# A perceiver block on one core: the last quarter of the last attention unit transposed on TensorE, four weight pairs loaded at once, and layer norms placed ahead of split halves

## The chip, the cores and the metric

The kernel runs on one core of a Trainium2 chip. The metric is the device time of one execution in microseconds, the median of several runs. The core's engines work side by side, each through its own queue in order: TensorE (PE in the profile; PEld is its weight load), VectorE (DVE), ScalarE (ACT), GpSimd (POOL) and SyncE (SP, which here only issues DMAs).

## The reference, cut to what matters

Three layers with residuals are computed for 512 tokens of width 1024: a cross attention whose queries, keys, values and attention weights are rounded to 8-bit levels, a causal self attention with rotary positions, and a feed-forward layer with 4-bit weights.

```python
x = x + xattn(layernorm(x), ctx, ...)   # 8192 keys, 16 heads of 64; then @ Wp + bp
x = x + attn(layernorm(x), ...)         # 4 sequences of 128, 16 heads; Wq, Wk, Wv, Wo
x = x + ffn(layernorm(x), ...)          # gate and up 1024 -> 2816, silu(gate) * up, down, rms norm

# inside xattn
attn = softmax(q @ k.T)                 # per head
attn = round(attn / s).clip(0, 255) * s # s = max(attn) / 255 of each row
out  = attn @ v
```

## The kernel before, in words

**Stages.** Up to about 1503 us keys and values of the 8192 context rows are projected and quantised. From 1503 to about 2166 us the cross attention runs in 64 units, one for each head `h` and each tile `t` of 128 tokens. Then come ten "parts" (`PARTS`), each a product of the 512 tokens with one 1024 x 512 half of a weight: parts 0 and 1 are the two halves of Wp, 2 the first half of Wv, 3 to 6 halves of Wq and Wk, 7 the second half of Wv, 8 and 9 the halves of Wo. From about 2503 us the feed-forward part runs: 22 rounds of gate and up, then down.

**A unit of the attention.** Its 8192 keys are eight groups of 1024 (`g`). `scores` makes the scores of a group; `exponentials` makes 4096 of them at a time into int16 levels `a`. The levels, read as the bits of a 16-bit float, must be transposed before they multiply the values. Quarters 0 and 2 of the keys are transposed by PE (`transposes`, two 16-bit levels moved as one 32-bit word, L830, copied to SBUF by ACT or DVE at L836), quarters 1 and 3 (`DMA_KC`) by DMA (`dma_transposes`, L845, issued on SP). `values` (L858) multiplies them. The loop over steps `s` writes the order out: `transposes` runs LAG_T = 12 and `values` LAG_V = 18 steps after `scores`. After the last scores only the tail of the last units is left; into its steps `FIRST_AT` puts eight single products of part 0 (`first_step`, L941).

**The parts.** From `with tc.manual_schedule()` on, an agenda fixes the order: `do(step, function, ...)` notes a time for each piece, and `perform` issues the pieces in the order of these times, so they are the order of every engine's queue, and not a time that anything waits for. A step is one k-chunk of 128 of one product; a part has 32 steps, `g = s + 8 t` is where tile `t` of a part begins and `e = g + 8` where it ends.

Weights come in pairs of k-chunks. `load_pair` loads 512 KB into one of two buffers `w_raw` (SP, L1028), `split_pair_hi` splits off the high part on ACT (`sw_h`, L155), `split_pair` the low part and the difference on DVE (`sw_l`, `sw_d`, L158 and L159), with six buffers of each. Three products of reduced precision then stand for one of full precision (`product_step`, L1100, accumulators `acc_a` and `acc_b`, two of each). The tokens are split in the same manner into `x3` (high, low, difference). Part 0 is the exception: it is done in full precision (L941), while `first_split` and `first_difference` (L1072) prepare the split tokens for part 1.

After parts 1 and 9 a tile is joined to the residual (L1111, L1112), its statistics are taken (L1126), and `normalise` writes the norm `xn` (L1131 to L1137). Later `xn_transposes` transposes it on PE (L1080, eight transposes into two PSUM tiles `pt` of three), takes the high halves on ACT (L155) and the low halves and differences on DVE (L158, L159, four instructions); `scale_low` scales the low part on ACT (L1087). Before the change each tile's `xn_transposes` stood 7.5 steps after the tile's end, which is just before the next tile's last half step and so before its norm:

```python
do(e + 0.4, normalise, t)
do(e + 7.5, xn_transposes, t)
do(e + 8.35, scale_low, t)
```

`first_gate_up` (L1253) is the first gate and up product of the feed-forward part; it needs the split norms of all four tiles. After the agenda, pools for the feed-forward part are opened where the pools of the parts were; `load_ffn` loads a weight (`fw_raw`, L1378) and splits it at once (`fw_h`, `fw_l`, `fw_d`). In this last section the order on the engines is found by a scheduler.

Of the kernel before, what the change touches and what calls it, by code (L numbers as in the profile page):

```python
# [34 lines left out]
F32 = mybir.dt.float32  # L35
# [11 lines left out]
P = 128  # L47
# [8 lines left out]
KC = 2048  # L56
# [7 lines left out]

FIRST_AT = (5, 6, 7, 14, 15, 17, 17, 17)
DMA_KC = (1, 3)
# [20 lines left out]
def tile_perceiver(  # L87
# [646 lines left out]
    with tc.tile_pool(name="at_e", bufs=1) as at_e, tc.tile_pool(  # L734
# [8 lines left out]
        for i in range(2):  # L743
            nc.vector.tensor_scalar_mul(sqs[:, i], sq, 1.0 - 2.0 * i)
        vqs = {}

# [77 lines left out]
        def transposes(n, g):  # L824
# [9 lines left out]

            copy = nc.scalar.copy if n < len(units) - 2 or g < 2 and n < len(units) - 1 else nc.vector.tensor_copy
            copy(aT, pt.bitcast(I32))  # L836
# [3 lines left out]
        def dma_transposes(n, c):  # L840

            at_key = c * KC % EC
            a = state[n]["a"][c * KC // EC][:, at_key : at_key + KC].bitcast(F16)
            aT = at.tile([P, KC // P, P], F16, name="aT_d", tag="aT_d", bufs=3)
            nc.sync.dma_start_transpose(out=aT, in_=a)  # L845
            for g in range(KC // SC):
                state[n]["aT", KC // SC * c + g] = [
                    aT[:, g * (SC // P) + i, :] for i in range(SC // P)
                ]

        def values(n, g):
# [105 lines left out]
        with tc.manual_schedule():  # L957
            for s in range(n_steps + LAG_V):
# [4 lines left out]
                if g == NSC // NEC and 1 <= n <= len(units):  # L963
                    dma_transposes(n - 1, DMA_KC[0])
                if g == 0 and 2 <= n <= len(units) + 1:
                    dma_transposes(n - 2, DMA_KC[1])
# [17 lines left out]
                if at_step(s - LAG_V):  # L984
                    values(*at_step(s - LAG_V))
                for fn, *args in meanwhile.get(s - n_steps, ()):
                    fn(*args)
# [33 lines left out]
    def load_pair(h, kp):  # L1021

        raw = sa_f.tile([P, 2, 512], F32, name="w_raw", tag="w_raw", bufs=2)
        if h < len(PARTS):
# [148 lines left out]
    def rotary_transposes(h, t, tag, bufs):  # L1173
        f = live.pop(("f", h, t))
        pt = sa_ps.tile([P, 4, P], F32, name="pt", tag="pt", bufs=3)
        for i in range(4):
            nc.tensor.transpose(pt[:, i, :], f[:, ts(i, P)], ident)
        fT = live[tag, t] = sa_f.tile([P, 4, P], F32, name=tag, tag=tag, bufs=bufs)
        nc.scalar.copy(fT, pt)
# [95 lines left out]
    with tc.manual_schedule():  # L1275
# [10 lines left out]
        for h, (w, n) in enumerate(PARTS):  # L1286
            s = PART * h

            if h > 0:
                for kp in range(NC // 2):  # L1290
                    at = s + {1: (-28, -22, -16, -10), 2: (-37, -33, -6, -3)}.get(h, (-26, -16, -6, -3))[kp]
                    do(at - 9.5, load_pair, h, kp)
                    do(at - 2.5, split_pair_hi, h, kp)
                    do(at + 0.5, split_pair, h, kp)
# [12 lines left out]
            for t in range(NT):  # L1307
# [17 lines left out]
                elif h == 1:  # L1325
                    do(e + 0.2, join_residual, h, t, n)
                    do(e + 0.3, stats, t, 1)
                    do(e + 0.4, normalise, t)
                    do(e + 7.5, xn_transposes, t)
                    do(e + 8.35, scale_low, t)  # L1330
                elif h in (2, 7):
# [38 lines left out]

    with tc.tile_pool(name="ff_t", bufs=2) as ff_t, tc.tile_pool(name="ff", bufs=1) as ff:
        hT = [ff.tile([P, 512], F32, name=f"hT{j}", tag=f"hT{j}") for j in range(NI)]
        ss = ff.tile([P, NT, 2], F32, name="ss")

        def load_ffn(src, n):

            raw = ff_t.tile([P, C], F32, name="fw_raw", tag="fw_raw")
            nc.sync.dma_start(out=raw.rearrange("p (i n) -> p i n", n=n), in_=src)  # L1378
# [18 lines left out]
        def split_inner(pool, j):  # L1397
# [178 lines left out]
```

## Time and profile before

| | us |
|---|---|
| median of 3 runs | 2870.38 (2868.08 to 2871.28) |
| the profiled execution | 2872.01 |
| its span | 2870.2 |
| PE busy | 2661.8 (93%) |
| DVE busy | 2421.4 (84%) |
| ACT busy | 1266.0 (44%) |
| end of the last score on DVE | 2147.3 |
| last product with the values | 2166 |
| first product of part 1 | 2198.2 |
| first product of part 2 | 2230.8 |
| first gate and up product | 2490.25 |
| first product of the loop of the feed-forward part | 2503 |

Times within the execution are counted from the start of its span. The busy shares are means over stages with different limits; what a change in one stage is worth is read from that stage. In a row of the timeline the bracket at the end gives the engine's idle time before the row and the instruction that ended it.

### The profile page before, as it was taken

Reading aid. Unit: us, or ns where it says so; the run is one execution under the profiler, and the core shown is the slowest. Engines: PE = TensorE matmul, PEld = TensorE weight load, DVE = VectorE, ACT = ScalarE, POOL = GpSimd, SP = SyncE. Lnnn points to the kernel's source line nnn. Section 1 sums busy time; section 2 is a strip of 40 time slices with the busy share of each in tenths; the row PEclk is TensorE's granted clock in tenths of the full one; section 3 lists DMA queues with packets and bytes.
Section 4 is the critical chain, followed back from the end, with each engine's and each line's share of the span. In section 5 each row is a group of like instructions: output and inputs, shape, how many; then the busy total and the mean of one; then the engine's idle time right before and its main releaser. Section 6 shows DMA issues by size and latency. Waiting matters only on the chain.

```text
span 2870.2 us, 41035 instructions
## 1 busy us (share of the span) xinstructions
PE 2661.8 (93%) x15480; PEld 2065.8 (72%) x15480; DVE 2421.4 (84%) x3959; ACT 1266.0 (44%) x1400; POOL 455.9 (16%) x608
## 2 busy tenths in 40 slices
PE   8999999999999999999997778877778899899998
PEld 3788888888888888888874555555555677688886
DVE  6899999555699988889879999999996898776674
ACT  4211212121323333333218999999993244333332
POOL 0011111000012222222122333223311000000000
PEclk9999999999999999999998999999999999899999
DMA  5555566222447776777437888778774221122222
GB/s 187 174 194 200 200 212 209 99 90 101 136 119 206 190 194 182 194 180 195 112 90 150 159 168 163 162 152 157 153 145 137 88 78 60 52 96 96 91 93 96
DMA packets 452710, 413.17 MB, mean 144 GB/s; under 512 B 356952, under 2 KB 361624, under 8 KB 452512
## 3 DMA queue, kind: packets, MB, share of 16 engines
q1 hardware_dynamic: 404928, 252.22, 35.9%
q0 software_dynamic: 46528, 157.29, 17.0%
q8 instruction: 121, 1.98, 0.3%
q10 hardware_dynamic: 1056, 1.05, 0.2%
q14 instruction: 77, 0.63, 0.1%
HBM read 220.14 MB, written 104.34 MB: 113 GB/s over the span
## 4 chain that ended last, share of the span: by engine, by line
PE 72%; DVE 19%; issue 4%; POOL 2%; DMA 1%; ACT 1%; DVEq 0%; ACTq 0%; SPq 0%; POOLq 0%
PE kv_a L342 33%; PE kv_b L342 16%; DVE e L787 13%; PE acc_a L1100 3%; PE gate_a L165 3%; PE up_a L165 3%; PE y_a L1463 3%; PE q_ps L292 2%; POOL sk L760 2%; PE acc_b L1100 2%; PE up_b L165 1%; PE gate_b L165 1%; PE y_b L1463 1%; PE a_pt L830 1%; PE sc L780 1%
## 5 line engine op out<-in xcount | busy, mean ns | idle before, releaser
L342 PE MATMUL kv_a<-w_h,c_h 128*128 128x512 f32 x2048 | 806.4, 394 | 0.0
L342 PE MATMUL kv_a<-w_l,c_l 128*128 128x512 f32 x2048 | 806.0, 394 | 0.2 <-ACT w_l L246 0.2
L342 PE MATMUL kv_b<-w_d,c_d 128*128 128x512 f32 x2048 | 806.0, 394 | 0.0
L787 DVE CUSTOM_DVE_ANT_0 e<-sc,sk 128x1024 f32<-128x1024 f32 x512 | 593.6, 1220 | 11.4 <-PE sc L780 10.3
L815 ACT ACTIVATE a<-e,m,sqs 128x4096 int16<-128x4096 f32 x128 | 486.9, 3804 | 27.9 <-DVE m L804 27.6
L342 PEld LDWEIGHTS kv_a<-w_l,c_l 128*128 128x128 f32 x2048 | 384.8, 188 | 89.6 <-ACT w_l L246 0.6
L342 PEld LDWEIGHTS kv_a<-w_h,c_h 128*128 128x128 f32 x2048 | 384.9, 188 | 88.9 <-issue 0.2
L342 PEld LDWEIGHTS kv_b<-w_d,c_d 128*128 128x128 f32 x2048 | 384.8, 188 | 88.9 <-DVE c_d L159 0.3
L155 ACT ACTIVATE c_h<-c_raw 128x1024 fp32r<-128x1024 f32 x128 | 135.1, 1056 | 424.2 <-PE kv_a L342 417.0
L356 DVE SCALAR_TENSOR_TENSOR f<-kv_a,bkv 128x512 f32<-128x512 f32 x256 | 175.8, 687 | 163.4 <-PE kv_a L342 162.7
L780 PE MATMUL sc<-kt,qT 64*128 64x512 bf16 x1024 | 207.0, 396 | 103.6 <-DVE mx L787 99.1
L581 ACT CAST kst<-kT 128x512 bf16<-128x512 int16 x128 | 89.4, 699 | 313.6 <-DMA kT<-ki 313.2
L830 PE MATMUL a_pt<-ident,a 128*128 128x128 f32 x1024 | 178.0, 299 | 20.8 <-ACT a L815 16.1
L357 DVE SCALAR_TENSOR_TENSOR f<-kv_b,f 128x512 f32<-128x512 f32 x256 | 176.7, 690 | 20.3 <-DVE f L356 0.9
L760 POOL PARTITION_BROADCAST sk<-sk_row x120 | 142.7, 1297 | 314.1 <-DVE mx L787 314.1
L830 PEld LDWEIGHTS a_pt<-ident,a 128*128 128x128 f32 x1024 | 113.8, 147 | 87.3 <-ACT a L815 48.3
L780 PEld LDWEIGHTS <-qT 64*128 64x128 bf16 x1024 | 74.9, 93 | 131.7 <-issue 101.3
L158 DVE TENSOR_TENSOR fw_l<-fw_raw,fw_h 128x1024 fp32r<-128x1024 f32 x64 | 78.2, 1222 | 99.8 <-ACT fw_h L155 99.6
L158 DVE TENSOR_TENSOR c_l<-c_raw,c_h 128x1024 fp32r<-128x1024 f32 x128 | 155.7, 1217 | 4.8 <-ACT c_h L155 4.4
L159 DVE SCALAR_TENSOR_TENSOR c_d<-c_l,c_raw 128x1024 fp32r<-128x1024 f32 x128 | 156.3, 1221 | 2.3
L155 ACT ACTIVATE fw_h<-fw_raw 128x1024 fp32r<-128x1024 f32 x64 | 67.7, 1060 | 174.6 <-PE y_a L1463 72.0
L548 ACT CAST vq<-vi 128x1024 f16<-128x1024 int16 x64 | 66.9, 1046 | 170.7 <-DVE vi L541 135.8
(204 smaller groups left out, 4110.1 us busy)
## 6 DMA issues: line engine op xcount, KB each, us to landing
c_raw<-in_ctxT SPq DMA_DIRECT2D x128, 512.0 KB, 3.6
v_d<-f POOLq DMA_DIRECT2D x64, 512.0 KB, 3.1
vl<-v_d POOLq DMA_DIRECT2D x64, 512.0 KB, 4.2
gu_d<-w_ffn POOLq DMA_DIRECT2D x44, 512.0 KB, 3.1
fw_raw<-gu_d SPq DMA_DIRECT2D x42, 512.0 KB, 3.2
k_d<-kst POOLq DMA_DIRECT2D x128, 128.0 KB, 3.5
vq_d<-vq POOLq DMA_DIRECT2D x32, 512.0 KB, 5.0
kt<-k_d SPq DMA_DIRECT2D x64, 256.0 KB, 3.5
```

Source lines behind the costliest of these rows:

```text
L155: nc.scalar.mul(hi, src, 1.0 - 0.5 / UP)
L158: nc.vector.tensor_tensor(lo, src, hi, ALU.subtract)
L159: nc.vector.scalar_tensor_tensor(df, lo, -1.0 - UP, src, ALU.mult, ALU.add)
L165: nc.tensor.matmul(ps, lhsT=lhs(i, k), rhs=rhs(i, k), start=(k == 0 and i != 1), stop=(k == NC - 1 and i != 0),)
L342: nc.tensor.matmul(ps, lhsT=tokens[s][i][:, k, :], rhs=w3[s < KT][k][i][:, ts(n, 512)], start=(k == 0 and i != 1), stop=(k == NC - 1 and i ...
L356: nc.vector.scalar_tensor_tensor(f, a, 1.0 + 1.0 / UP, bias[s < KT][n], ALU.mult, ALU.add)
L357: nc.vector.scalar_tensor_tensor(f, b, -1.0 / UP, f, ALU.mult, ALU.add)
L760: nc.gpsimd.partition_broadcast(tile_of_scales(h, g), sks_at[h][32 * c : 32 * c + 1, ts(half, SC)], channels=P)
L780: nc.tensor.matmul(ps[:, ts(i, 512)], lhsT=qT[rows, h, ts(t, P)], rhs=kts[h, g // 2][rows, ts(g % 2, 512)], start=True, stop=True,)
L787: nc.vector.tensor_tensor_reduce(out=state[n]["e"][-1][:, ts(g % (NSC // NEC), SC)], in0=ps, in1=sks_at[h, g], scale=1.0, scalar=LOWEST, o ...
L815: nc.scalar.activation(a, st["e"][c], AF.Exp, bias=st["m"], scale=sqs[:, 0, t, h : h + 1], accum_out=sums[h][:, t, c : c + 1],)
L830: nc.tensor.transpose(pt[:, i, :], a[:, at_word + P * i : at_word + P * i + P], ident)
```

## The change

- The fourth quarter of the last unit is no longer transposed by DMA. `last_transposes` multiplies it on PE with a 16-bit identity (`ident16`, copied once before the attention), in four groups of four blocks; the levels come out as fractions in PSUM and are scaled back to int16, groups 0 and 2 on DVE, 1 and 3 on ACT. The copy of group 5 of the last unit goes from DVE to ACT.
- Two of the first steps of part 0 move four steps forward (`FIRST_AT`, 14 and 15 to 10 and 11).
- All four weight pairs of part 1 are loaded together ahead of the other pieces; pairs 2 and 3 get one buffer of their own, which is later the place of the transposed queries `qT`, now one tile in place of four. The splits of pairs 1 and 2 of part 1, and of pairs 0 and 1 of part 2, get other times.
- `xn_transposes` and `scale_low` get later times in parts 1 and 9, so that the norm of the next tile comes first.
- The feed-forward pools are cut differently: `fw_raw` and the first ten tiles `hT` get pools of their own.

```diff
-FIRST_AT = (5, 6, 7, 14, 15, 17, 17, 17)
+FIRST_AT = (5, 6, 7, 10, 11, 17, 17, 17)
...
+        ident16 = small.tile([P, P], F16, name="ident16", tag="ident16", bufs=1)
+        nc.scalar.copy(ident16, ident)
...
-            copy = nc.scalar.copy if n < len(units) - 2 or g < 2 and n < len(units) - 1 else nc.vector.tensor_copy
+            by_act = n < len(units) - 2 or (n, g) == (len(units) - 1, 5) or g < 2 and n < len(units) - 1
+            copy = nc.scalar.copy if by_act else nc.vector.tensor_copy
...
+        def last_transposes(q):
+            n, c = len(units) - 1, DMA_KC[1]
+            at_key = c * KC % EC + 512 * q
+            a = state[n]["a"][c * KC // EC][:, at_key : at_key + 512].bitcast(F16)
+            if q == 0:
+                aT = at.tile([P, KC // P, P], I16, name="aT_l", tag="aT_d", bufs=3)
+                state["last"] = aT
...
+            pt = at_ps.tile([P, 4, P], F32, name="a_pt", tag="a_pt")
+            for i in range(4):
+                nc.tensor.matmul(
+                    pt[:, i, :], lhsT=a[:, ts(i, P)], rhs=ident16, start=True, stop=True
+                )
+            scale = nc.vector.tensor_scalar_mul if q % 2 == 0 else nc.scalar.mul
+            scale(state["last"][:, ts(q, 4), :], pt, F16_UNITS)
...
-                if g == 0 and 2 <= n <= len(units) + 1:
+                if g == 0 and 2 <= n <= len(units):
                     dma_transposes(n - 2, DMA_KC[1])
...
+                if n == len(units) + 1 and 1 <= g <= KC // 512:
+                    last_transposes(g - 1)
...
-        raw = sa_f.tile([P, 2, 512], F32, name="w_raw", tag="w_raw", bufs=2)
+        if h == 1 and kp >= 2:
+            if kp == 2:
+                live["raw"] = sa_f.tile([P, 2, 2, 512], F32, name="w_raw2", tag="qT")
+            raw = live["raw"][:, kp - 2]
+        else:
+            raw = sa_f.tile([P, 2, 512], F32, name="w_raw", tag="w_raw", bufs=2)
...
-        fT = live[tag, t] = sa_f.tile([P, 4, P], F32, name=tag, tag=tag, bufs=bufs)
+        if tag == "qT":
+            if t == 0 and h == 3:
+                live["q"] = sa_f.tile([P, NT, 4, P], F32, name=tag, tag=tag)
+            fT = live[tag, t] = live["q"][:, t]
+        else:
+            fT = live[tag, t] = sa_f.tile([P, 4, P], F32, name=tag, tag=tag, bufs=bufs)
...
-                    at = s + {1: (-28, -22, -16, -10), 2: (-37, -33, -6, -3)}.get(h, (-26, -16, -6, -3))[kp]
-                    do(at - 9.5, load_pair, h, kp)
+                    at = s + {1: (-28, -24, -13.8, -10), 2: (-35, -31, -6, -3)}.get(h, (-26, -16, -6, -3))[kp]
+                    do(-9.3 if h == 1 else at - 9.5, load_pair, h, kp)
...
-                    do(e + 7.5, xn_transposes, t)
-                    do(e + 8.35, scale_low, t)
+                    do(e + 9.5, xn_transposes, t)
+                    do(e + 10.4, scale_low, t)
...
-                        do(e + 7.5, xn_transposes, t, True)
-                        do(e + 8.35, scale_low, t)
+                        do(e + (9.5, 9.5, 8.6, 7.5)[t], xn_transposes, t, True)
+                        do(e + (10.4, 10.4, 8.7, 8.35)[t], scale_low, t)
...
-    with tc.tile_pool(name="ff_t", bufs=2) as ff_t, tc.tile_pool(name="ff", bufs=1) as ff:
-        hT = [ff.tile([P, 512], F32, name=f"hT{j}", tag=f"hT{j}") for j in range(NI)]
+    with tc.tile_pool(name="ff_t", bufs=2) as ff_t, tc.tile_pool(
+        name="ff_a", bufs=1
+    ) as ff_a, tc.tile_pool(name="ff_raw", bufs=2) as ff_raw, tc.tile_pool(name="ff", bufs=1) as ff:
+        inner_pool = [ff_a if j < EARLY + 2 else ff for j in range(NI)]
+        hT = [inner_pool[j].tile([P, 512], F32, name=f"hT{j}", tag=f"hT{j}") for j in range(NI)]
...
-            raw = ff_t.tile([P, C], F32, name="fw_raw", tag="fw_raw")
+            raw = ff_raw.tile([P, C], F32, name="fw_raw", tag="fw_raw")
...
-            df = ff.tile([P, 512], F32R, name=f"h3_d{j}", tag=f"hT{j}")
+            df = inner_pool[j].tile([P, 512], F32R, name=f"h3_d{j}", tag=f"hT{j}")
```

More of the change, by code (lines that the diff above doesn't have):

```diff
@@ L849, in dma_transposes @@
                 ]
+        def last_transposes(q):
[5 more added lines that the diff above has]
+                state["last"] = aT
+                for g in range(KC // SC):
+                    state[n]["aT", KC // SC * c + g] = [
+                        aT.bitcast(F16)[:, g * (SC // P) + i, :] for i in range(SC // P)
+                    ]
+            pt = at_ps.tile([P, 4, P], F32, name="a_pt", tag="a_pt")
[5 more added lines that the diff above has]
+            scale(state["last"][:, ts(q, 4), :], pt, F16_UNITS)
         def values(n, g):
```

## The prediction

> **What bounds the kernel now.** I read the busy times by stretch first, then what TensorE (PE) waited for from the end of the attention on, then single rows of the timelines around those waits. By stretch (the columns are busy us and instructions of PE, its weight loads, DVE, ACT, POOL, then the granted clock, the DMA share and GB/s):
>
> ```profile
> 2151.00:2204.00 53.00, 43.86 (x233) 25.14 (x233) 30.19 (x33) 22.19 (x25) 13.48 (x11) 0.90 0.59 187
> 2204.00:2257.00 53.00, 44.70 (x194) 35.92 (x195) 43.05 (x65) 14.48 (x21) 0.00 (x0) 0.94 0.18 56
> 2257.00:2459.00 202.00, 193.35 (x1054) 157.62 (x1054) 180.56 (x243) 81.82 (x202) 11.79 (x8) 0.99 0.23 76
> 2459.00:2503.00 44.00, 30.26 (x131) 24.23 (x130) 27.13 (x43) 11.91 (x19) 0.00 (x0) 0.81 0.14 48
> 2503.00:2738.00 235.00, 235.00 (x1008) 189.03 (x1007) 162.83 (x192) 84.41 (x115) 0.00 (x0) 1.00 0.26 91
> ```
>
> The change touches 2151 to 2257 (end of attention, parts 0 to 2) and 2459 to 2503 (last part, first gate and up). There PE is idle 9.1, 8.3 and 13.7 us, at reduced clock, while the feed-forward loop after it is full: PE 235.00 of 235.00. So a microsecond by which that loop starts earlier is a microsecond of the whole. Who holds PE up there:
>
> ```profile
> PE pt L1080 <- DVE xn L1137: 21.0, 6, 6.5
> PE acc_a L941 <- issue: 5.1, 1, 5.1
> PE acc_b L1100 <- DVE x_d L1072: 2.5, 1, 2.5
> PE av L858 <- DMA aT_d<-a: 1.8, 1, 1.8
> ```
>
> and the rows with those waits in brackets:
>
> ```profile
> 2162.69 0.64 PE L858 MATMUL av<-vq,aT_d 128*128 128x64 f16 x16 [1.79 <-DMA aT_d<-a]
> 2181.84 5.75 PE L941 MATMUL acc_a<-wp,xoT 128*128 128x512 f32 x8 [5.07 <-issue]
> 2205.03 2.56 PE L1100 MATMUL acc_b<-sw_d,x_d 128*128 128x512 f32 x8 [2.54 <-DVE x_d L1072]
> 2222.06 1.06 PE L1080 MATMUL pt<-ident,xn 128*128 128x128 f32 x8 [1.30 <-DVE xn L1137]
> 2230.01 1.06 PE L1080 MATMUL pt<-ident,xn 128*128 128x128 f32 x8 [1.29 <-DVE xn L1137]
> 2241.36 1.94 PE L1080 MATMUL pt<-ident,xn 128*128 128x128 f32 x8 [4.67 <-DVE xn L1137]
> 2479.90 1.94 PE L1080 MATMUL pt<-ident,xn 128*128 128x128 f32 x8 [6.00 <-DVE xn L1137]
> 2488.31 1.95 PE L1080 MATMUL pt<-ident,xn 128*128 128x128 f32 x8 [6.47 <-DVE xn L1137]
> ```
>
> One more 1.27 at 2467. The 5.07 is called issue, but the join of acc(0,0) frees the accumulator at 2181.73 on DVE (L1117); it stands behind x_l(0), that behind ACT's x_h(0), that behind the split of weight pair 2, whose load waits for its buffer:
>
> ```profile
> 2151.74 10.61 SPq L845 DMA_TRANSPOSE aT_d<-a  x2
> 2163.57 1.72 SPq L1028 DMA_DIRECT2D w_raw<-in_xWp  x2
> 2174.23 2.76 SPq L1028 DMA_DIRECT2D w_raw<-in_xWp  x2
> 2177.87 1.06 ACT L155 ACTIVATE sw_h<-w_raw 128x1024 fp32r<-128x1024 f32 x1 [5.28 <-DMA w_raw<-in_xWp]
> ```
>
> All these waits together are 30.4 us of 2870: that is the room.
>
> **The change part by part.**
>
> *Last quarter on PE.* One DMA transpose goes (its 3.82 us on SP, 2158.54 to 2162.36); 16 products with an fp16 identity and four scalings come. No row shows this product. Bounds: eight 128x64 fp16 products take 0.41 us, four fp32 transposes 0.66, so 0.8 to 2.6 for the 16; I take 1.1, nearer to the fp16 row. Each scaling is near an aT copy, 0.69 on DVE or 0.58 on ACT; both are nearly idle there. The wait of 1.79 is not for the removed transfer: it is for the second quarter, issued at 2151.74 and landing after 10.9 us, while wp and x load. It stays; but two first steps (0.94 each) now come before it, with three of the four groups. PE then reaches that point at about 2163.5, after the landing at 2162.65. So 1.8 goes, 1.1 comes: PE is at the last transposes of xo at 2167.8 instead of 2168.64, **0.8** gained. wp's second half lands 9.5 after 2148.7, at 2158.2, before the moved steps need it.
>
> *Four pairs at once.* SP has issued the second quarter at about 2158.4 (10.61 less the last 3.82), so the loads go out some 5 us earlier, pairs 2 and 3 in a buffer of their own (qT's slot, unused until part 3). The split of pair 2 moves behind the first two tiles' splits on ACT and DVE. I replay the queues with the trace's durations: xoT copies done at 2169.9; sw_h twice; DVE pairs 2 x 2.45; x_l(0) 1.22; join 0.68: the accumulator is free at 2177.5 instead of 2181.7. PE stands still 1.5 instead of 5.07, and is **4.2** ahead there (the 0.8 included). What is late next: the weights of part 2, pair 1, now stand between the differences x_d(0) and x_d(1) on DVE. In place of 2.54 before acc_b(1,0) I get 0.8 there and 3.0 before (1,1): **-1.3**.
>
> *Norms ahead, part 1.* Each transpose of xn moves behind two further steps (6 products of 0.234 = 1.4 us), and on DVE the norm of tile t+1 (join to xn, 3.85 us, L1111 to L1137) comes before the four split halves of tile t (2.75). That covers 1.30 and 1.29; the 4.67 becomes 0.9, plus 0.9 for a PSUM buffer of `pt` not yet split, and the join of (2,0), now behind the halves, holds up (2,2) by 2.7. 7.26 becomes 4.5: **+2.8**. Parts 3 to 8 get the same work in the same order; the replay carries the lead through unchanged.
>
> *Norms ahead, last part.* Replay, in the times of before, the front's lead not yet taken off: xn(1) at 2463.4, then the last weight pair (2.45) and the halves of tile 0, xn(2) at 2471, in time for PE, which comes to it at 2473. xn(3) is done at 2477.3 instead of 2488.2. But on ACT the scaling of tile 2 stands before x_h(3), so the first gate and up starts at about 2482.8 instead of 2490.25: 7.5, and with the trace's short wait inside it (5.23 for products worth 3.75 at full clock) **8**. Here the new pools matter: the first fw_raw loads stood behind the release of w_raw at 2469.43, their four DVE splits ahead of xn; now they wait for PE too and their splits come after x_d(3). A load takes 3.2, splitting one weight 1.06 + 2.4: ready near 2490 against the first gate at 2495. Cover 5 us; if gone, the excess is lost one to one.
>
> *Clock.* After a wait the trace shows half clock: 0.50 in 2182 to 2186, 0.52 in 2208 to 2210, 0.50 in 2242 to 2244; the waits of 1.3 left 1.00. The 8 records at 2181.84 took 5.75 against 3.5 for their like at full clock. I count 2.2 + 1.9 + 1.4 = 5.5 us lost so in the first region. [...] But here 2.54 was enough; so I charge two leftovers with 1.9 each: **+1.7**. At the end both versions run some products cold: 0.
>
> *At nothing:* the identity's copy (one ACT copy before the first exponentials), the query tile in one piece (same bytes and order), hT in another pool (same order in the loop).
>
> Sum: 4.2 - 1.3 + 2.8 + 8 + 1.7 = 15.4. The profiled execution took 2872.0 (span 2870.2), so 2856.6 there; it is 1.6 above the median, 2870.4, so the median forecast is **2855**.
>
> **Rivals.**
> *Only one side pays.* DVE does 43 of 53 us in parts 1 and 2, so it may be the bound: 30.4 us of waiting would merely change names. Then the end alone gives 8: 2862. If instead fw_raw is released late and eats the end's gain, the front's 7.4 alone: 2863. For it: 3.0 and 2.7 already reappear. Against: DVE itself waits some 15 us between 2168 and 2246, mostly for ACT, behind pair 2.
> *More than replayed.* The leftover waits don't arise and the clock stays up: of 30.4 + 5.5, 22 is won: 2848.
> *Nothing measurable.* The burst of 2 MB meets wp, x and the second quarter's transpose (DMA share above 1.0 at 2152 to 2164), so the weights land no sooner, and fw_raw costs the end: within 6 us of 2870.
> *Slower.* The pools of the feed-forward part are cut anew. If a tile there falls on one released later, the wait recurs in each of 21 rounds of fw_raw loads. The loop has no slack on PE; each microsecond per round costs 21. From 0.75 us per round it eats my 15.4; at 1.2 it gives 2880. Against it: the order of loads and splits in the loop and the number of buffers stay the same, and DVE has 72 us spare in 235.
>
> **How the numbers follow.** A measurement of this kernel tells 0.2% (5.7 us) from no change. Forecast 0.66, one side 0.17, more 0.05, nothing 0.05, slower 0.07. The first three are faster by over 0.2%, less a little of the one-sided case: faster 0.87, same 0.06, slower 0.07. The forecast's own bounds (identity products 1.5 either way, cold stretches 4, leftovers 3) give 2849 to 2861; to hold 8 in 10 with the one-sided case the range is 2847 to 2865.
>
> **What would show it.** Right: no DMA wait on av at the end; the wait before the first xoT step near 1.5; the 4.67, 6.00 and 6.47 gone or under 2.5; first gate near 2488. A second-quarter landing later than 2164, an accumulator wait over 4 in part 2, or a wait of gate_a for fw_h would show a step wrong; a feed-forward loop longer than 235 the slower rival.

## The result, and the profile after

The changed kernel took 2857.37 us (median of 5 runs, 2854.13 to 2859.43) against 2871.28 for the kernel before in the same comparison: a ratio of 0.9951, 95% interval 0.9937 to 0.9966. A second comparison, made with the last experiments, gave 2856.77 against 2873.02, a ratio of 0.9941 (0.9926 to 0.9955). So the change gains 14 to 16 us (the interval of the first comparison reaches from 10 to 18), more than the 0.2% that can be told; 2855 was forecast.

The profiled execution took 2854.13 us, with a span of 2852.4. The first view is the one that the prediction opened with: busy us and instructions of PE, its weight loads, DVE, ACT and POOL, the granted clock, the DMA share and GB/s. The stretches run between nearly the same places of the program as those shown of before: the third boundary lies ten products later in the program and the fourth six.

```profile
2147.40:2195.60 48.20, 41.22 (x249) 23.54 (x249) 29.12 (x32) 23.78 (x28) 13.89 (x11) 1.00 0.55 187
2195.60:2247.70 52.10, 47.45 (x204) 37.25 (x205) 46.27 (x68) 13.80 (x21) 0.00 (x0) 0.93 0.21 63
2247.70:2450.00 202.30, 192.31 (x1050) 156.98 (x1050) 180.35 (x244) 81.72 (x202) 12.74 (x8) 0.99 0.24 77
2450.00:2485.50 35.50, 28.38 (x125) 22.60 (x124) 26.57 (x42) 11.35 (x18) 0.00 (x0) 0.86 0.17 60
2485.50:2720.50 235.00, 235.00 (x1008) 189.03 (x1007) 162.77 (x192) 84.56 (x115) 0.00 (x0) 1.00 0.27 91
```

The first stretch went from 53.0 to 48.2 us and its clock from 0.90 to 1.00; the fourth went from 44.0 to 35.5, of which six products (1.4 us) are the boundary's. The feed-forward loop did not move, and the long third stretch hardly. What PE waits for, in total us, times and the longest (from 2140 on; some smaller rows and one that is as before are left out):

```profile
PE pt L1207 <- DVE f L1201: 9.8, 4, 4.9
PE pt L1110 <- DVE xn L1167: 5.5, 2, 4.5
PE acc_b L1130 <- DVE x_d L1102: 3.8, 2, 3.5
...
PE acc_a L1288 <- ACT x_h L155: 1.8, 1, 1.8
PE acc_a L1130 <- DVE v L1141: 1.7, 1, 1.7
PE acc_a L964 <- DMA wp<-in_xWp: 1.6, 1, 1.6
...
PE acc_a L964 <- issue: 1.6, 1, 1.6
```

The waits for xn fell from 21.0 to 5.5 us, the 5.1 of the first xoT step to 1.6, and the wait of av for the DMA transpose is gone. The wait for a rotary f now heads the list, and one of 1.6 for the weights wp of part 0 is new; it is taken up below. The rows behind the list, each with its wait in brackets:

```profile
2156.83 0.39 PE L868 MATMUL a_pt<-ident,a 128*128 128x128 f16 x4
...
2173.76 3.67 PE L964 MATMUL acc_a<-wp,xoT 128*128 128x512 f32 x8 [1.56 <-issue]
...
2196.61 3.78 PE L1130 MATMUL acc_b<-sw_d,x_d 128*128 128x512 f32 x8 [3.54 <-DVE x_d L1102]
...
2201.46 0.79 PE L1130 MATMUL acc_b<-sw_d,x_d 128*128 128x512 f32 x1 [0.21 <-DVE x_d L1102]
...
2264.27 1.08 PE L1207 MATMUL pt<-ident,f 128*128 128x128 f32 x4 [4.92 <-DVE f L1201]
...
2468.32 1.09 PE L1110 MATMUL pt<-ident,xn 128*128 128x128 f32 x4 [4.48 <-DVE xn L1167]
...
2472.51 5.49 PE L1288 MATMUL acc_a<-x_h,sw_h 128*128 128x512 f32 x16 [1.78 <-ACT x_h L155]
```

**How the executions are compared.** Two profiles of unlike executions should not be laid side by side by absolute time. The kernel after was already 3.56 us ahead at 2148.06, at the end of the exponentials of the last unit's first half, ahead of all changed code but the one copy of `ident16` (before: 2151.62). In its second profile that place was at 2152.75, and over the fourteen profiles it lay from 2146.9 to 2154.4, so the lead belongs to the one execution. I therefore count from that place: the *front* runs from it to the transposes of the last rotary f of part 6, the *end* from there to the first gate and up product (2490.09 before; the 2490.25 in the table ahead is 0.16 late), and the last column gives the loop's first gate, counted from it too.

| kernel | first xoT step | first rotary f | front | end | first gate |
|---|---|---|---|---|---|
| before | 30.2 | 122.0 | 240.7 | 97.8 | 351.2 |
| after | 25.7 | 116.2 | 233.9 | 90.6 | 337.2 |
| after, second profile | 25.3 | 114.8 | 233.3 | 90.6 | 336.7 |
| front alone | 25.6 | 116.1 | 234.4 | 97.9 | 344.7 |
| end alone | 29.5 | 123.8 | 240.5 | 90.6 | 343.8 |
| end, norms alone | 31.2 | 125.1 | 242.8 | 95.8 | 351.3 |
| four pairs alone | 26.7 | 120.6 | 237.1 | 97.8 | 347.6 |
| norms of part 1 alone | 30.1 | 118.4 | 237.2 | 97.8 | 347.7 |
| last quarter alone | 29.1 | 121.2 | 237.8 | 99.3 | 350.2 |
| after, pair 0 first | 25.8 | 115.0 | 233.6 | 90.9 | 337.4 |
| after, differences first | 25.7 | 112.9 | 230.6 | 91.0 | 334.2 |
| after, scaling later | 25.7 | 116.0 | 233.6 | 88.5 | 334.3 |
| after, rows later | 25.8 | 112.4 | 229.5 | 92.1 | 334.4 |
| after, all three | 25.7 | 110.0 | 225.2 | 90.4 | 328.0 |

The profiles of one unchanged stretch spread: the front of the three kernels that left it as before is 240.5 to 242.8, and the stretch between the first and the last rotary, with the same work in the same order, took 116.5 to 118.8 us over the kernels that left its additions in place. Most of the second spread is TensorE's clock: behind the wait for the first rotary it ran at a clock of 0.50 for 3.4 us, which by that clock costs half of it, 1.7, in nine of these twelve profiles, and stayed at 1.00 in end alone, four pairs alone and last quarter alone. The fronts of these three are so much shorter without any merit of the edit (the last section has the reason). A difference of 1 us in the front is therefore not read from one profile; single waits repeat better: the 3.54 before acc_b lay within 3.53 and 3.55 in the six profiles that have it. By the profiles of before and after, the total of 17.8 us is 3.6 before the changed code, 13.9 in the changed stretches and 0.3 behind them.

### The profile page after: what moved, and what is told of

The parts are those of the page before. It is cut to its first block, busy times and chain, and to the rows that moved or that the text cites. A ratio compares the mean times of both kernels' runs of the same rounds, so it can differ in the third digit from the quotient of the medians.

```text
span 2852.4 us, 41096 instructions
## 1 busy us (share of the span) xinstructions
PE 2652.6 (93%) x15496; PEld 2059.5 (72%) x15496; DVE 2421.2 (85%) x3960; ACT 1267.0 (44%) x1404; POOL 455.7 (16%) x608
## 4 chain that ended last, share of the span: by engine, by line
PE 70%; DVE 21%; issue 4%; POOL 2%; ACT 1%; DMA 1%; DVEq 0%; ACTq 0%
PE kv_a L342 32%; PE kv_b L342 16%; DVE e L789 14%; PE acc_a L1130 3%; PE up_a L165 3%; PE gate_a L165 3%; PE y_a L1503 3%; POOL sk L762 2%; PE q_ps L292 2%; PE acc_b L1130 1%; PE up_b L165 1%; PE gate_b L165 1%; PE y_b L1503 1%; PE a_pt L832 1%; DVE sw_l L158 1%
## 5 line engine op out<-in xcount | busy, mean ns | idle before, releaser
L158 DVE TENSOR_TENSOR fw_l<-fw_raw,fw_h 128x1024 fp32r<-128x1024 f32 x64 | 78.3, 1224 | 99.4 <-ACT fw_h L155 99.3
```

Of the source, the lines that this page charges most:

```text
L158: nc.vector.tensor_tensor(lo, src, hi, ALU.subtract)
```

## The experiments

### The two sides apart

Front alone: the changed kernel with the last part's times and the pools of the feed-forward part put back. End alone: the kernel before with these two edits only.

```diff
-                        do(e + (9.5, 9.5, 8.6, 7.5)[t], xn_transposes, t, True)
-                        do(e + (10.4, 10.4, 8.7, 8.35)[t], scale_low, t)
+                        do(e + 7.5, xn_transposes, t, True)
+                        do(e + 8.35, scale_low, t)
...
-    with tc.tile_pool(name="ff_t", bufs=2) as ff_t, tc.tile_pool(
-        name="ff_a", bufs=1
-    ) as ff_a, tc.tile_pool(name="ff_raw", bufs=2) as ff_raw, tc.tile_pool(name="ff", bufs=1) as ff:
+    with tc.tile_pool(name="ff_t", bufs=2) as ff_t, tc.tile_pool(name="ff", bufs=1) as ff:
...
```

> The changed kernel with the end as it was before: norms of the last part at their old times, pools of the feed-forward part as before. Two stretches are compared: the front, from the end of the last unit's first-half exponentials to the last rotary transposes of part 6 (240.7 us before, 233.9 after), and the end, from there to the first gate-and-up product (97.8 before, 90.6 after). Theory (the two places add): front 233.9, end 97.8, time 6.8 under before, 2864.5. Rival 'only one side pays, DVE is the bound in front': the lead of the front is lost again, front near 240, time near 2871. Rival 'the parts need each other': neither stretch comes out as in the changed kernel.

> The kernel before with the end alone changed: norms of the last part at their new times, and the new pools of the feed-forward part. Theory: front 240.7, end 90.6, time 7.1 under before, near 2864. Rival 'the end pays only with the lead of the front': end 94 or more, time 2868 or more. Rival 'the new pools cost in the feed-forward loop': the loop of 235 us grows and eats the 7.

Measured: front alone 0.9980 of before (0.9971 to 0.9988; 2867.09 against 2871.60), with front 234.4 and end 97.9. End alone 0.9981 (0.9973 to 0.9990; 2867.25), with front 240.5 and end 90.6. Each stretch is that of the changed kernel where the edit was made, and that of the kernel before where it was not. By these stretches the sides add, and neither needs the other; both times lie under before, with intervals that leave no change out. That ends the rival "only one side pays". The medians are less clear: the two sides give 4.5 and 4.4 us, 8.9 together, where the whole gave 13.9 and 16.3. Their intervals reach to 8.3 and 7.8, so they allow the full sum but do not show it; where the rest would have gone is open. From the loop's first gate to the end of the span it is 367.4 us before, 367.1 after and 367.0 with the end alone, so the slower rival, a wait that recurs in the loop, does not exist.

### The end without its pools

The kernel before with only the times of the last part's norms changed (the first two pairs of lines above, the other way round).

> The kernel before with only the times of the norms in the last part changed; pools of the feed-forward part as before, so the first fw_raw loads land early and their four split rows on DVE (4 x 1.22 = 4.9 us) stand ahead of a norm. Theory (DVE is the bound of this stretch): end 90.6 + 4.9 = 95.5, time near 2869. Rival (pools are worth nothing, the wait of PE for xn was an order of PE alone): end 90.6, time near 2864.

Measured: 1.0000 (0.9991 to 1.0009), end 95.8. Of the end's 7.2 us only 2.0 remain; this profile also lost 1.7 us to the clock there (last section), so some 3.7 would be left without that, while the time shows no gain at all. The DVE timeline of this kernel, just ahead of the third norm:

```profile
2476.67 1.23 DVE L158 TENSOR_TENSOR fw_l<-fw_raw,fw_h 128x1024 fp32r<-128x1024 f32 x1
2477.81 0.21 DVE L1131 BATCH_NORM_AGGREGATE ln_mv<-ln_st 128x2 f32<-128x12 f32 x1
2477.93 1.18 DVE L158 TENSOR_TENSOR fw_l<-fw_raw,fw_h 128x1024 fp32r<-128x1024 f32 x1
2479.02 0.15 DVE L1133 TENSOR_SCALAR ln_rstd<-ln_mv 128x1 f32<-128x1 f32 x1
2479.08 1.22 DVE L159 SCALAR_TENSOR_TENSOR fw_d<-fw_l,fw_raw 128x1024 fp32r<-128x1024 f32 x1
2480.22 0.16 DVE L1135 RECIPROCAL ln_rstd<-ln_rstd 128x1 f32<-128x1 f32 x1
2480.29 1.21 DVE L159 SCALAR_TENSOR_TENSOR fw_d<-fw_l,fw_raw 128x1024 fp32r<-128x1024 f32 x1
2481.41 0.81 DVE L1137 TENSOR_SCALAR xn<-x,ln_mv,ln_rstd 128x1024 f32<-128x1024 f32 x1
```

Four splits of feed-forward weights, 4.84 us, stand between the rows of one norm: with the old pools the weights land early, and DVE takes what is ready. The pools are not bookkeeping; by holding the loads back they take 3.5 us (95.8 less 90.6, less the clock's 1.7) to 4.8 (the four rows) off the path.

### The three edits of the front, one at a time

Each on the kernel before. Four pairs alone:

```diff
+        if h == 1 and kp >= 2:
+            if kp == 2:
+                live["raw"] = sa_f.tile([P, 2, 2, 512], F32, name="w_raw2", tag="qT")
+            raw = live["raw"][:, kp - 2]
...
-                    at = s + {1: (-28, -22, -16, -10), 2: (-37, -33, -6, -3)}.get(h, (-26, -16, -6, -3))[kp]
+                    at = s + {1: (-28, -24, -13.8, -10), 2: (-35, -31, -6, -3)}.get(h, (-26, -16, -6, -3))[kp]
-                    do(at - 9.5, load_pair, h, kp)
+                    do(-9.3 if h == 1 else at - 9.5, load_pair, h, kp)
```

> The kernel before with only the four pairs of part 1's weights loaded at once (pairs 2 and 3 in qT's place) and their and part 2's split times as in the changed kernel; the last quarter by DMA and the norms as before. Theory (each lead is carried on): PE 3.5 ahead at the first xoT step (wait 5.07 becomes about 2.5), about 3 ahead after part 1's first accumulator wait, front 237 to 238, time near 2868. Rival (DVE is the bound in parts 1 and 2): the lead goes into longer waits for xn, which stood at 1.3, 1.3 and 4.67; front 240 or more, time near 2871. A second rival: without the quarter on TensorE the queue reaches the loads 3.8 us later, so the wait of 5.07 hardly falls.

Measured: 0.9994 (0.9986 to 1.0003). The wait before the first xoT step is 1.63 instead of 5.07 and PE is 3.5 ahead there, so the fourth quarter's DMA does not matter for it. But the lead is carried on only in part. Before acc_b PE now stands 3.55 instead of 2.54, as after, and behind that it ran at half clock for 5.2 us instead of 3.4: at the first rotary the lead is 1.4. The 3.6 at the end of the front hold the 1.7 of clock that before lost at the first rotary and this profile did not. So the rival, that the lead goes into longer waits, is right for more than half of it. The time alone says little: its interval reaches from 4 us gained to 1 lost.

Norms of part 1 alone:

```diff
-                    do(e + 7.5, xn_transposes, t)
-                    do(e + 8.35, scale_low, t)
+                    do(e + 9.5, xn_transposes, t)
+                    do(e + 10.4, scale_low, t)
```

> The kernel before with only the norms of part 1 moved (transposes of xn and the scaling two steps later). Theory (the norm of one tile covers the split of the last): the wait of 4.67 for xn falls to about 1.1 and those of 1.3 vanish, about 2.4 come back as a wait for the row splits and for an accumulator, front 240.7 - 2.2 = 238.5, time near 2869. Rival (a tuned order of DVE work, where each row moved makes another one late): front 240 or more, time 2871 or more.

Measured: 0.9993 (0.9984 to 1.0003), front 237.2, so 3.5 gained, all of it before the first rotary; 2.2 was expected. The waits are 0.95 for xn, 0.69 for a split row and 1.66 for an accumulator, 3.3 in place of 7.3. Those are the rows that were expected, and the rival, that each moved row makes another late by as much, is out for this step.

Last quarter alone: `last_transposes`, its copy and scaling, `ident16`, and `FIRST_AT` as in the changed kernel.

```diff
-FIRST_AT = (5, 6, 7, 14, 15, 17, 17, 17)
+FIRST_AT = (5, 6, 7, 10, 11, 17, 17, 17)
...
-                if g == 0 and 2 <= n <= len(units) + 1:
+                if g == 0 and 2 <= n <= len(units):
...
+                if n == len(units) + 1 and 1 <= g <= KC // 512:
+                    last_transposes(g - 1)
```

> The kernel before with only the last quarter on TensorE (with the moved first steps). Theory (the accumulator of tile 0, not PE, ends the wait before the first xoT step, and it hangs on the load of weight pair 2, which waits for its buffer): PE is 1.0 earlier at the last transposes, waits that much longer, 6.1 in place of 5.07, and the front stays at 240.7: alone it is worth nothing. Rival (SP is free of a transposition of 3.8 us earlier, so the weights land earlier): the front falls by 1 to 3.8.

Measured: 0.9989 (0.9980 to 0.9997), front 237.8. My expectation failed. PE came to the first xoT step 1.2 earlier and waited 5.08, not 6.1. The ACT timelines say why, first of before, then of this kernel:

```profile
2169.62 1.07 ACT L1050 COPY xoT<-pt 128x512 f32<-128x512 f32 x2
2170.58 2.02 ACT L155 ACTIVATE sw_h<-w_raw 128x1024 fp32r<-128x1024 f32 x2
2177.87 1.06 ACT L155 ACTIVATE sw_h<-w_raw 128x1024 fp32r<-128x1024 f32 x1 [5.28 <-DMA w_raw<-in_xWp]
```

```profile
2166.96 1.07 ACT L1075 COPY xoT<-pt 128x512 f32<-128x512 f32 x2
2167.92 2.01 ACT L155 ACTIVATE sw_h<-w_raw 128x1024 fp32r<-128x1024 f32 x2
2175.30 1.06 ACT L155 ACTIVATE sw_h<-w_raw 128x1024 fp32r<-128x1024 f32 x1 [5.37 <-DMA w_raw<-in_xWp]
```

The first two splits stand on ACT right behind the copies of PE's last transposes, with no gap, and pair 2's load waits for these splits to free its buffer. The chain that ends the wait begins at PE, so what PE gains ahead of it moves the whole chain. The rival's reason, an SP free earlier, is not it either: the third load still starts only when the buffer comes free. With the four pairs the quarter is worth 26.7 less 25.6 (four pairs alone against front alone), 1.1 us. Its 16 products took four groups of 0.23 from start to start, 0.9 us. Of the 2.9 by which the front is shorter here, 1.7 is the clock behind the first rotary, which stayed at 1.00. (Of the 99.3 of the end in this profile 1.7 is clock too, lost there.)

At the first rotary the three alone are 1.4, 3.6 and 0.8 ahead of before, 5.8 in sum; the front alone is 5.9 ahead there, the whole change 5.8 and, in its second profile, 7.2.

### The misplaced wait: 3.54 us before acc_b

The changed kernel with pair 0 of part 2 split ahead of the last tile's split on ACT, and then, besides, with pair 1's split behind x_d(1) on DVE:

```diff
-... 2: (-35, -31, -6, -3) ...
+... 2: (-36.6, -31, -6, -3) ...
```

```diff
-... 2: (-35, -31, -6, -3) ...
+... 2: (-36.6, -27, -6, -3) ...
```

The loads of these pairs and their high parts move with them.

> The changed kernel with one ACT row moved: the high part of part 2's weight pair 0 is split ahead of the split of the last tile, not behind its scaling; the order on DVE, PE, POOL and SP stays. Theory (the 3.54 us wait before acc_b(1,0) is DVE standing 2.07 us for ACT's scaling and weight split, behind a DVE row that took 2.20): x_d(0) comes 2 us earlier, the wait is 1.5, front 231.9, time near 2855. Rival (the wait is made of DVE's own rows, slowed by GpSimd's additions): the slowed row only moves, the wait stays over 3, front 233 or more.

> The changed kernel with pair 0 of part 2 split early on ACT, as in the kernel before this one, and on DVE pair 1's split behind the difference of tile 1, x_d(1). The two waits before acc_b were 1.38 and 2.2 when only pair 0 was moved, 3.54 and 0.21 in the changed kernel. Theory (they are order on DVE): now 1.4 and under 0.3, front 231.5, time 2 under the changed kernel. Rival (DVE is the bound of parts 1 and 2: from x_l(3) to the norms it has no gap): PE's lead goes into longer waits for xn, for the accumulator or for the rotary, front 233 or more.

Measured, the first: 0.9944 (0.9932 to 0.9957). The wait before acc_b(1,0) fell to 1.38 as expected, but 2.25 appeared before acc_b(1,1), where there had been 0.21; the front is 233.6, the same as after. Only the place of the wait changed, from one difference of part 1 to the next. The second: 0.9930 (0.9919 to 0.9942), front 230.6, 3.2 less than after; the waits before acc_b were 1.38 and 1.51 for x_d and 0.70 for a weight, 3.6 in sum against 3.75 after. The waits hardly shrank, but none was long, and the gain is clock. From the first product of part 1 on, the stretches of after and then of the second of these kernels:

```profile
2188.78:2216.00 27.22, 23.46 (x97) 18.15 (x95) 23.81 (x32) 7.59 (x10) 1.00 (x1) 0.87 0.12 39
```

```profile
2191.82:2219.00 27.18, 24.30 (x111) 18.93 (x110) 25.47 (x37) 7.86 (x12) 1.00 (x1) 1.00 0.13 39
```

The clock of these 27 us rose from 0.87 to 1.00, and 111 instructions ran in place of 97. The eight acc_b products took 3.78 us behind the wait of 3.54, and 2.13 behind the wait of 1.38. In after the clock was 0.50 from 2195.92 to 2202.75, so the five products behind these eight were slow as well; in the second of these kernels it stayed at 1.00 until the first rotary.

Ahead of the wait, in after, GpSimd adds a bias to x, and DVE's rows beside it are long:

```profile
2182.41 7.37 POOL L1072 TENSOR_TENSOR x<-x,row 128x512 f32<-128x512 f32 x4 [4.60 <-DMA x<-in_x]
2185.24 2.17 DVE L159 SCALAR_TENSOR_TENSOR sw_d<-sw_l,w_raw 128x1024 fp32r<-128x1024 f32 x1
2188.66 2.20 DVE L1094 TENSOR_TENSOR x_l<-xoT,x_h 128x1024 fp32r<-128x1024 f32 x1
```

Rows of their kind take 1.22. No run moved these additions, so their part in the wait is read from the rows and not tested.

### The end's last wait

The changed kernel with the scaling of tile 2 behind the high parts of tile 3:

```diff
-                        do(e + (10.4, 10.4, 8.7, 8.35)[t], scale_low, t)
+                        do(e + (10.4, 10.4, 15.6, 8.35)[t], scale_low, t)
```

> The changed kernel with one ACT row of the last part moved: the scaling of tile 2's low part goes behind the high parts of tile 3. Theory (the 1.78 us wait of the first gate-and-up product is for x_h(3) behind that scaling): the wait falls to about 0.7, the end from 90.6 to about 89.5, time 1 under the changed kernel. Rival (what is late next are the low and difference rows of tile 3 and the two fw_h, all moved 1 us back): gate-and-up starts earlier but the loop's first gate does not, the stretch from the one to the other grows from 12.8 to 13.9.

Measured: 0.9946 (0.9932 to 0.9959); the end is 88.5 instead of 90.6, and from gate and up to the loop's first gate 12.3 instead of 12.8. ACT, first of after, then of this kernel:

```profile
2470.92 1.06 ACT L1117 ACTIVATE x_l<-x_l 128x1024 fp32r<-128x1024 f32 x1 [2.81 <-DVE x_d L159]
2471.88 1.07 ACT L155 ACTIVATE x_h<-pt 128x512 fp32r<-128x512 f32 x2
```

```profile
2469.47 0.60 ACT L155 ACTIVATE x_h<-pt 128x512 fp32r<-128x512 f32 x1 [1.40 <-PE pt L1110]
2470.79 0.60 ACT L155 ACTIVATE x_h<-pt 128x512 fp32r<-128x512 f32 x1 [0.72 <-PE pt L1110]
```

In the changed kernel ACT stood 2.81 us for DVE with finished transposes waiting behind it. Without the scaling in front, x_h(3) starts 2.4 earlier, when the first half of its transposes is done, and gate and up starts on that half. I had expected 1.1, for I counted from the second half; and nothing late followed.

### The wait that was not foreseen: 4.92 us for the first rotary

The changed kernel with GpSimd's eight additions of the output bias taken from parts 3 and 5 to part 7:

```diff
-            if h in (3, 5):
-                m = (h - 3) // 2
-                do(s + 8, keep, ("bo", m), load_bias, abo, m)
-                for t in range(NT):
-                    do(s + 9, lambda t, m: add_row(t, m, rows["bo", m]), t, m)
+            if h == 7:
+                for m in range(2):
+                    do(s + 2 + m, keep, ("bo", m), load_bias, abo, m)
+                    for t in range(NT):
+                        do(s + 3 + m, lambda t, m: add_row(t, m, rows["bo", m]), t, m)
```

> The changed kernel with GpSimd's eight bias additions of the attention output (x<-x,row) taken from parts 3 and 5 to part 7, where TensorE waits for nothing. Theory (a DVE row with two inputs in SBUF stands while GpSimd adds: two rot rows took 2.89 instead of 0.76, two more 1.63 instead of 0.69 in part 3): the first rotary f is ready some 4 us earlier, the wait of 4.92 falls to 1 to 2.6, front 230 to 231.5, and rows of DVE in part 7 are slowed instead, with no wait of TensorE, so time near 2854. Rival (the wait of 4.92 is the length of the chain join, rot, add itself): the wait stays over 4, front 233 or more. Second rival: the same microseconds are lost in part 7, so the front shrinks and the end grows from 90.6 to 93 or more.

Measured: 0.9942 (0.9929 to 0.9954). DVE's rows of the first rotary f with GpSimd's beside them, of after:

```profile
2257.82 5.76 POOL L1072 TENSOR_TENSOR x<-x,row 128x512 f32<-128x512 f32 x4 [68.03 <-DMA row<-in_abo]
```

```profile
2257.90 2.89 DVE L1192 TENSOR_TENSOR rot<-f,cs 128x256 f32<-128x256 f32 x2
2260.83 1.63 DVE L1198 TENSOR_TENSOR f<-f,cs 128x512 f32<-128x512 f32 x1
2262.49 1.63 DVE L1201 TENSOR_TENSOR f<-f,rot 128x512 f32<-128x512 f32 x1
```

and of this kernel, where the additions no longer stand there:

```profile
2261.42 0.76 DVE L1192 TENSOR_TENSOR rot<-f,cs 128x256 f32<-128x256 f32 x2
2262.22 0.69 DVE L1198 TENSOR_TENSOR f<-f,cs 128x512 f32<-128x512 f32 x1
2262.94 0.69 DVE L1201 TENSOR_TENSOR f<-f,rot 128x512 f32<-128x512 f32 x1
```

6.15 us of rows became 2.14, and PE's wait went from 4.92 to 1.01. So 3.9 of it are GpSimd's, or 2.9 by the second profile of after, which waited 3.93 (there the rows took 5.2). Behind the short wait the clock stayed at 1.00. But the second rival is right in part. The additions came early enough to meet the last rotary f of part 6:

```profile
2377.39 1.67 DVE L1198 TENSOR_TENSOR f<-f,cs 128x512 f32<-128x512 f32 x1
2379.09 1.63 DVE L1201 TENSOR_TENSOR f<-f,rot 128x512 f32<-128x512 f32 x1
2380.65 1.27 DVE L1230 TENSOR_TENSOR sa_sc<-sa_scp,mask 128x512 f32<-128x512 f32 x2
```

GpSimd's eight began at 2377.25 and ran 12.86 us; PE waited 4.65 there instead of 2.73, and the end grew by 1.5: behind that wait the clock was 0.50 from 2380.68 to 2384.10, which is 1.7. The rows show which operations suffered here. The third has one input in PSUM and one in SBUF, and it took 1.27 for two, as elsewhere (1.28), with GpSimd at work. Rows with both inputs in SBUF were stretched, from 0.69 to 1.6; so was one small row with a single input, from SBUF to SBUF (L1235, TENSOR_SCALAR, at 2383.21: 1.15 instead of 0.17). What held these rows up, no run shows.

### All three moves together

The changed kernel with differences first, scaling later, and the additions in part 7 with their rows loaded six steps later (`s + 8 + m` and `s + 9 + m`); and the changed kernel itself for the comparison.

> The changed kernel with the three moves together: differences of part 1 ahead of pair 1's split, scaling of tile 2 in the last part behind tile 3's high parts, and GpSimd's eight additions in part 7, their rows loaded six steps later than in the kernel that tried this alone, so that they come behind the last rotary of part 6. Theory (each took one wait of TensorE and they lie in different places): first rotary transposes from 116.2 to about 109.5 after the end of the first-half exponentials, the end from 90.6 to 88.5, the loop's first gate from 337.2 to about 328.5, time 9 under the changed kernel, near 2848. Rival (DVE is the bound from part 1 to the rotary, so what two of them give is one sum): first rotary 112 to 113, first gate 331 to 332, time near 2851.

> The changed kernel itself, as it is, for the comparison on one chip and for a second profile of it. Theory (the stretches are the program's, the 3.6 us by which its first profile was ahead before the changed code are that execution's): front 233.9, end 90.6, first gate 337.2 after the end of the first-half exponentials, but that end anywhere from 2148 to 2154; time near 2857. Rival (the change makes the attention before it faster): that end at 2148 again.

Measured: all three 2846.75, 0.9906 of before (0.9890 to 0.9921), against 0.9941 (0.9926 to 0.9955) for the changed kernel beside it: 10.0 us faster, and the intervals do not meet. The first rotary is at 110.0, the loop's first gate at 328.0; 109.5 and 328.5 were expected, so the three lie in different places and add. (The end of 90.4 in this profile holds 1.7 us of lower clock.) PE's waits in this kernel:

```profile
PE pt L1110 <- DVE xn L1167: 6.0, 3, 4.5
PE pt L1207 <- DVE f L1201: 4.9, 3, 2.7
```

The rotary's 9.8 is 4.9. The longest that is left is the 4.5 for xn(3) in the last part. DVE has no gap longer than 0.3 us there, from 2448.89 to 2470.83 in the profile of after, so less work on DVE or another order of it would have to help; neither was tried.

## Why the prediction was right

The sum was 15.4; the comparisons gave 13.9 and 16.3. By stretch it was 7.4 for the front and 8 for the end. The front measured 241.3 less 233.8, so 7.5 (the means of three profiles with the old front and four with the new; 6.9 against before alone), the end 97.8 less 90.6, so 7.2.

- *Last quarter, 0.8.* Measured 1.1, with products of 0.9 where 1.1 was put (the two terms of the forecast, 1.8 and 1.1, leave 0.7). The nearest row of the trace, the fp16 products, was the right one to take. No wait of av for DMA is left. The new wait for wp, 1.62 in front of the first step of part 0, is no loss: that step began 4.1 us behind the mark of the table, and 4.0 in before, where PE came late instead, at a clock of 0.50 from 2151.89 to 2155.30. So a part of the first stretch's rise in clock gained nothing.
- *Four pairs, 4.2 ahead, wait 1.5.* Measured 4.5 ahead and 1.56. The chain (accumulator, join, x_l(0), x_h(0), pair 2, its buffer) was read rightly.
- *The step behind it, -1.3, was right as a sum and wrong in place.* I put 0.8 before acc_b(1,0) and 3.0 before (1,1); it was 3.54 and 0.21. The replay used 1.22 for every DVE row of that size, though the trace of before has one of 2.18 (sw_d, 2194.17) while GpSimd added there. In after, while GpSimd added the bias to x (2182.41 to 2189.78), the two split rows of the fourth pair took 1.57 and 2.17 and x_l(3) 2.20: 2.3 us more on the one chain that mattered. With ACT's scaling and split behind it, x_d(0) came late and x_d(1) in time.
- *Norms of part 1, +2.8, with 4.5 of waits left.* Alone they gave 3.5. The waits left were 1.07, 0.69 and 1.66, that is 3.4; the mis-sized term is the accumulator's, 2.7 put and 1.66 measured.
- *"The replay carries the lead through unchanged" failed at the first rotary.* The wait there was 2.63 before, 4.92 after, and 3.93 in the second profile, so 1.3 to 2.3 us of the lead are lost. GpSimd's additions met that f in both kernels: the rot and f rows took 5.2 us before and 6.15 after, for 0.9 of it. The other 1.4 is that PE, now earlier, comes to f 3.0 us after its join began, where it was 4.3 before: DVE, busy with the weights ahead of the join, did not come forward by as much as PE. More from the norms than forecast made up for it.
- *Clock, +1.7: nearly right, by two errors that cancel.* In before PE ran at 0.50 for 4.18, 3.41 and 2.69 us behind its three long waits. Half of that, 5.1 us, is lost; 5.5 was counted. Two leftover waits were charged with 1.9 each. One of them occurred, the 3.54, and behind it PE ran at 0.50 until 2202.75, for 5.9 us without the wait of 0.21: 3.0 lost, not 1.9. Behind the other, 1.66, the clock stayed up. So 2.1 was won. That the one drop cost more than its price and the other nothing is luck.
- *Last part, 8.* Measured 7.2. Set on the last rotary of before, the first gate and up product began at 2482.85, where the replay had 2482.8. But inside it two errors of 1.2 cancel: xn(3) was done at 2478.5 instead of 2477.3, and what stands behind it took 4.3 instead of 5.5. The wait for xn(3) is 4.48, over the 2.5 that was named as the sign of being right, as DVE is full there. The half microsecond on top of the replay's 7.5 was misread: the row of 5.23 holds no wait, its clock was 0.50 until 2493.22, and it was so after the change until 2475.82. The 1.78 behind ACT's scaling was foreseen; it was an avoidable loss of 2.1. That the pools matter was right: without them 3.5 to 5.2 of the 7.2 are gone, by the four split rows of the argument. The loads were issued at 2470.80, the first fw_h ran at 2474.09, and no gate waited for it.
- *"First gate near 2488".* It was at 2485.31 in an execution that was 3.56 ahead before the change, so at 2488.9 in the times of before.

So the chains were read rightly, but that the sum came so close is in part luck: several of its terms are off by about 1 us and cancel. The main errors were durations taken as constants, in two places where another engine was at work, and one price for every drop of the clock.

## What to carry to other kernels

Before crediting a wait that is removed, follow the chain that ended it back to where it starts: one that starts at the waiting engine moves with it, and one that is ordered on another engine can be shortened by moving a single instruction there. Take a row's duration from the trace with its neighbours: DVE rows with two SBUF inputs that took 0.69 and 1.22 us alone took 1.63 and 2.20 here beside GpSimd's additions, so bookkeeping additions on an idle GpSimd belong where DVE is not the next thing waited for. Compare two profiles from a common event just ahead of the change, not from the start of the span.

## What the runs showed of the hardware that was not expected

The same wait does not always cost the same. Before the last rotary of part 6 PE stood 2.70 to 2.74 us in thirteen of the fourteen profiles here. In ten of them the clock of the next 17 us was 1.00, in three it was 0.90, which is 1.7 us lost: 98 instructions of PE in place of 109. A longer wait can even be the cheaper one: before the first rotary PE stood 2.63 us in before and the clock fell, and 3.40 in last quarter alone and it did not. Slices of 3.41 us around these two waits (which ended at 2273.61 and 2271.38), first of before, then of last quarter alone; the first sum is PE's busy time, and the last three numbers are the clock, the DMA share and GB/s:

```profile
2271.36:2274.77 3.41, 1.16 (x7) 1.06 (x8) 2.10 (x3) 0.49 (x1) 1.56 (x1) 1.00 0.02 5
2274.77:2278.18 3.41, 3.41 (x10) 2.63 (x8) 3.20 (x6) 0.10 (x1) 0.00 (x0) 0.50 0.00 0
```

```profile
2266.15:2269.57 3.42, 1.83 (x8) 1.12 (x6) 3.38 (x3) 0.00 (x0) 3.42 (x4) 1.00 0.25 95
2269.57:2272.98 3.41, 1.60 (x9) 1.44 (x10) 2.11 (x2) 0.59 (x1) 1.11 (x1) 1.00 0.00 0
2272.98:2276.39 3.41, 3.41 (x16) 2.74 (x15) 3.20 (x7) 0.00 (x0) 0.00 (x0) 1.00 0.00 0
```

The slices are not chosen at will. In each profile all changes of the clock from 2140 to 2600 us lie on one raster of 3.41 us (in before 2151.89, 2155.30, 2179.20, 2186.02, 2206.50 and so on). Against the place from which I count, the raster lies differently from profile to profile: one of its edges is 0.27 us behind that place in before, 0.07 in after, and 0.32 ahead of it in the second profile of after. In before the wait fell mostly into one slice of the raster, in which PE was busy for a third of the time, and the next slice ran at half clock. In the other the wait was shared by two slices, each busy for about half, and the clock stayed. The busy share sorts the other waits at these two places too. At the first rotary twelve profiles have a wait of 2.63 to 4.92: nine lost the clock, each behind a slice that was busy for 0.42 of its time or less; three kept it, with no slice under 0.47. Of the thirteen before the last rotary, three lost it, behind slices of 0.31 or less, and ten kept it, with none under 0.425.

A slice need not be idle throughout for this: in before a wait of 2.63, most of it in a slice that was busy for 0.34, was enough. The busy share is not the whole measure: elsewhere between 2140 and 2500 us four slices that were busy for 0.46 to 0.63 were followed by half clock too. No run set the place of the raster; it varied by itself. So in sizing a leftover wait of 2 to 3 us in this kernel, 1.7 more is a possible cost, not a sure one.
